# First attention of a four-layer kernel: closing token tiles by pairs inside the attention's last group, and writing the routing's column marks in four pieces

## The chip, the cores and the metric

The kernel runs on one core of a Trainium2 chip. The metric is the device time of one execution in microseconds, and where several runs are given, their median. All engines of the core take part: TensorE (PE; its weight loads are listed apart as PEld), VectorE (DVE), ScalarE (ACT), GpSimd (POOL) and SyncE (SP), which issues most of the DMA transfers. Lines such as L235 are lines of the kernel before the change.

## The reference

Four layers, each an attention and a feed-forward part, with a residual and a layer norm after each part. The state x has 1024 tokens of 256 numbers. Only the first layer matters here; what follows it is the same in both kernels.

```python
x = L0_attn_x
x = _layernorm(x + _L0_attn_ref(x, Wq, Wk, Wv, Wo, lam), axis=-1)   # (x - mean) / sqrt(var + 1e-5)
x = _layernorm(x + _L0_ffn_ref(x, Wr, Wg, Wu, Wd), axis=-1)
...
# _L0_attn_ref: 16 heads of 128 on 4 key heads, rotary angles, a window of 64 tokens;
# the probabilities are relu(softmax(q1 k1) - lam * softmax(q2 k2)), made to sum to 1
# _L0_ffn_ref: 8 experts of 256 x 256, two for each token
router_logits = jnp.einsum('bsh,he->bse', hidden_states, Wr)          # 1024 x 8
topk_logits, selected = jax.lax.top_k(router_logits, 2)
router_probs = jax.nn.softmax(topk_logits, axis=-1)
for e in range(8):
    w_e = jnp.where(selected == e, router_probs, 0.0).sum(axis=-1, keepdims=True)
    g = jnp.clip(jax.nn.silu(x @ Wg[e]), -7, 7)
    out = out + ((g * (x @ Wu[e])) @ Wd[e]) * w_e
```

## The kernel before

x lies in SBUF as eight tiles of 128 tokens (`k.x`), beside a transposed copy (`k.xT`) that the products read. The stages run one after the other (`STAGES`, L2145): attn0, ffn0, attn1 and so on. Each opens pools of its own, and a tile of a new pool whose memory was an old tile's waits until the old one was last read.

**attn0** (L513) goes through 32 units, four groups of four heads (g) by eight token tiles (t), in an order written out by hand (`in_order`). In one turn of its loop three units are worked on: unit i gets its scores (L666 and L676 on PE, the largest value by L684 on DVE, eight exponentials L692 on ACT), unit i-1 its difference of the two softmaxes (L700 to L708 on DVE, four relus L712 on ACT, the division L720 on POOL), and unit i-3 its product with the values: four transposes L729 on PE, a copy to `pt` L731 on ACT, L735 on PE, a copy to `ot` L741 on ACT, the output product L747 on PE, and L235 on DVE, which adds the result to x. While there are groups left, each turn also makes rotated queries and keys of the next half group (L154 on PE, L570 and L572 on DVE, L577 and L578 on POOL). In the last turns there is nothing left to make, and the units' own chain is alone. For g = 3 tile t of x is final when unit (3, t) has been added.

Loads are issued by SP in the order of the program. At the start these are x, the first keys, the rotary tables, weights, `lam` (L551), more weights, and then small tensors that later stages need, the first of them `bq` of attn1 (L1002), which DVE scales early (`scaled_bq`, L1004), ahead of the first unit's L684.

After the loop, `k.layernorm()` (L188) norms x by halves of four tiles: `bn_stats` and `bn_aggr` (L204, L205) for each tile, a square root on ACT (L222) and a reciprocal on DVE (L223) for four tiles together, then L208 on each tile. The function `four_layers` then turns all eight tiles with four calls of `transpose_two` (transposes L173 on PE, a copy L180 on DVE).

**ffn0** (L764) sends tokens to experts. Each token is put into two of 23 blocks of 128 slots, blocks belonging to one expert each.

- x is stored to DRAM by halves (`moe_rows`, L781), and the experts' weights are loaded: 24 transfers of 256 KB into `gu` (L787) and `wd` (L790), all on SP's queue. The second half's store stands in that queue behind the first eight of them. The first transfer waits for the last product of attn0 with the value tiles (L735), whose memory `gu` takes over.
- Routing: logits of all eight tiles (16 products of 128x8, L161 by way of `project_rows`), copied out by L817; the two largest for each token (`max` and `max_index`, L819 and L820); `chosen` as floats (L823); `mine` marks each token's experts (L824), `taken` sums them (L830). Two sorts of products (L833, L837) rank the tokens of an expert; L844 to L870 make of this the slot of each token, as a block and a column in it.
- `is_column` (L874, 128x2048 marks) and `is_block` (L879 to L886) are the operands of 16 products (L892) whose sum is the list of tokens by slot. `tokens` (L899) and `experts` (L909) come from it.
- 23 gathers by POOL (L228) fetch the rows of x by `tokens`, and then the blocks run: transposes (L927), the two hidden products (L938), the down product (L957).

The probabilities of a token's two experts (`prob`, L912 to L917) are not needed before the end of ffn0.

A later stage, attn3, already closes its tiles by pairs with a generator called `close`, with the inverse root as a power on POOL (`power`, L212: L215 on DVE, then L216 on POOL). The trace therefore has rows of such a closing.

Of the kernel before, what the change touches and what calls it, by code (L numbers as in the profile page):

```python
# [31 lines left out]
P = 128  # L32
T = 1024
NT = T // P
D = 256
# [477 lines left out]
def attn0(k, a):  # L513
# [89 lines left out]

    odd, even = [], []

    def make_values(t):
        vt = k.tile("v", [P, 512])
        ps = k.bank()
        k.project_rows(ps, lambda c: wv[:, c, :], t * P)
        nc.scalar.copy(vt, ps)  # L610
        odd.append(vt)
        vt = k.tile("v", [P, 512])
        if t == 0:
            nc.gpsimd.memset(vt[:64], 0.0)
        else:
            nc.sync.dma_start(out=vt[:64], in_=odd[t - 1][64:])
        nc.sync.dma_start(out=vt[64:], in_=odd[t][:64])
        even.append(vt)

    runs = [(g, half) for g in range(4) for half in range(2)]  # L620
    with k.in_order():
# [4 lines left out]
        for i in range(len(units) + 3):  # L626
# [7 lines left out]
            if i < len(units):  # L634
                g, t = units[i]
                if t % 4 == 0:
                    for _ in ahead:
                        pass
                    at = i // 4 + 1
                    ahead = operands(*runs[at]) if at < len(runs) else iter(())  # L640
                    if t == 0 and 0 < g < 3:
                        load(g + 1)
                next(ahead, None)
                if g == 0:
                    make_values(t)
            next(ending, None)
            if i < len(units):
                made[i] = attn0_probs(k, t, g, queries[g, t // 4], keys[g], lam)
# [115 lines left out]
def ffn0(k, a):  # L764
# [6 lines left out]
    blocks = 2 * T // P + 7  # L771
    gu = k.tile("gu", [P, 8, NC, 512])
    wd = k.tile("wd", [P, 8, NC, D])
    rows = k.tile("dram", [T, D], tag="moe_rows")
    results = k.tile("dram", [blocks * P, D], tag="moe_results")
    wr = k.weights([P, NC, 8], a["L0_ffn_Wr"].rearrange("(c p) e -> p c e", p=P))
    ternary_tiles = list(ffn1_weights(k, a))
    for tile_ in ternary_tiles[:2]:
        next(tile_)
    for half in range(2):  # L780
        nc.sync.dma_start(  # L781
            out=rows[half * HALF : (half + 1) * HALF, :].rearrange("(t p) d -> p t d", p=P),
            in_=k.x[:, 4 * half : 4 * half + 4, :],
        )
# [7 lines left out]
    def small(shape, dtype=F32):  # L792
        return k.tile("route", shape, dtype)
# [21 lines left out]
    logits, top = small([P, NT, 8]), small([P, NT, 8])  # L815
    which = small([P, NT, 8], U32)
    nc.vector.tensor_copy(logits, ps)  # L817
# [3 lines left out]
    chosen, mine = small([P, 2, NT]), k.tile("route", [P, 2, NT, 8], tag="mine", bufs=1)  # L821
    for i in range(2):
        nc.vector.tensor_copy(chosen[:, i, :], which[:, :, i])  # L823
    nc.vector.tensor_tensor(  # L824
        mine, cols[:, :8].unsqueeze(1).unsqueeze(1).to_broadcast([P, 2, NT, 8]),
        chosen.unsqueeze(3).to_broadcast([P, 2, NT, 8]), ALU.is_equal,
    )
    taken = small([P, NT + 1, 8], BF16)
    nc.vector.memset(taken[:, NT, :], 0.0)
# [20 lines left out]
    for i, by in enumerate((1, 2, 4)):  # L850
# [28 lines left out]
    nc.vector.tensor_tensor(  # L879
        hit.rearrange("p k t b -> p (k t) b"),  # L880
# [8 lines left out]
        )  # L889
    ps = k.bank()[:, : 2 * blocks].rearrange("p (i b) -> p i b", i=2)  # L890
    for i in range(2 * NT):
        nc.tensor.matmul(  # L892
            ps, lhsT=is_column[:, i, :], rhs=is_block[:, i // NT, i % NT],
            start=i == 0, stop=i == 2 * NT - 1,
        )
    low = small([P, blocks])
    nc.vector.tensor_copy(low, ps[:, 0, :])
    tokens = k.tile("route", [P, blocks], I32, tag="tokens", bufs=1)
    nc.vector.scalar_tensor_tensor(tokens, ps[:, 1, :], float(P), low, ALU.mult, ALU.add)  # L899

    passed = k.tile("route", [P, blocks, 7], tag="passed", bufs=1)
    nc.vector.tensor_tensor(
# [8 lines left out]
    prob = k.tile("const", [P, 2, NT], tag="prob")  # L911
    p1, p2 = prob[:, 0, :], prob[:, 1, :]  # L912
    nc.vector.tensor_tensor(p2, top[:, :, 1], top[:, :, 0], ALU.subtract)
# [1245 lines left out]
def four_layers(ctx: ExitStack, tc: tile.TileContext, a, out):  # L2159
# [88 lines left out]
```

## Time and profile before

| | |
|---|---|
| runs | 2280.4, 2282.05, 2284.7 us; median 2282.05 |
| the profiled execution's own time | 2276.97 us |
| its span, from the first to the last instruction | 2275.3 us |
| PE busy | 2065.0 us (91%), mean granted clock 0.965 |
| DVE, ACT, POOL busy | 58%, 38%, 23% |
| attn0's loop ends (last L235) | 294.5 us |
| first gather (L228) | 316.1 us |
| first expert's product (L938) | 322.1 us |

The profiled execution lies 5.1 us below the median of the runs. Times within it count from the start of the span. In the view of the stretches, each row is a piece of time with the busy time (and number of instructions) of PE, PEld, DVE, ACT and POOL, then the granted clock of PE as a share of full speed, the share of the DMA engines that is busy, and GB/s. In the timeline, a row is a start, a duration, an engine, a line and what it writes from what; a bracket tells for how long the engine had been idle and what it waited for. In the chain of waits a row is a start, a duration and an operation, each following what released it.

### The profile page before, as it was taken

The page shows a single profiled execution, that of the slowest core. Times are in us where ns is not written, and L with a number is a line of the kernel's source. Part 1 is how long each engine was busy: PE and PEld are TensorE (multiplying, and loading weights), DVE is VectorE, ACT ScalarE, POOL GpSimd, SP SyncE. Part 2 cuts the span into 40 slices and gives each one's busy share as a digit, 9 for nine tenths or more (in the row PEclk, how much of TensorE's full clock was granted, in tenths as well). Part 3 has the DMA queues.
Part 4 walks back from the last instruction along what each step waited for, and adds up shares of the span by engine and source line. Part 5 has one row for each costly group of instructions (what it writes and reads, how often), then busy time and mean ns, then how long its engine had stood idle before and what let it go on. Part 6 is the DMA issues. An engine that isn't in the chain of part 4 may idle for free.

```text
span 2275.3 us, 25208 instructions
## 1 busy us (share of the span) xinstructions
PE 2065.0 (91%) x7955; PEld 1211.8 (53%) x7955; DVE 1325.2 (58%) x2687; ACT 856.9 (38%) x2230; POOL 528.2 (23%) x805
## 2 busy tenths in 40 slices
PE   8999769799999997988888999899998778999997
PEld 4666545466676665754434444466666444444443
DVE  5677646567776777456744444476767774222223
ACT  3666624443343433444452224544443321111111
POOL 4333221333333333402110001333333220000000
PEclk9999879899999999979999999999999989999999
DMA  4100054254545544105000010244445441111100
GB/s 160 36 10 29 29 169 121 65 136 110 139 112 151 151 111 117 38 28 177 2 2 10 28 29 1 48 90 111 96 103 112 104 95 39 37 40 44 30 2 19
DMA packets 200804, 166.74 MB, mean 73 GB/s; under 512 B 71680, under 2 KB 176192, under 8 KB 200672
## 3 DMA queue, kind: packets, MB, share of 16 engines
q1 hardware_dynamic: 191088, 140.07, 24.0%
q0 software_dynamic: 9584, 25.05, 3.7%
q8 instruction: 65, 1.06, 0.2%
q14 instruction: 67, 0.55, 0.1%
HBM read 68.72 MB, written 17.17 MB: 38 GB/s over the span
## 4 chain that ended last, share of the span: by engine, by line
PE 67%; DVE 15%; ACT 6%; DMA 4%; issue 4%; POOL 2%; SPq 1%; DVEq 0%; ACTq 0%; POOLq 0%
PE bank L154 23%; PE wide L307 8%; PE wide L332 8%; PE bank L298 7%; PE bank L161 4%; DVE turned L276 3%; ACT e L692 3%; PE bank L758 2%; DMA pt<-turned 2%; PE bank L1107 2%; PE bank L1544 1%; PE bank L938 1%; PE bank L1282 1%; DVE st L684 1%; PE bank L747 1%
## 5 line engine op out<-in xcount | busy, mean ns | idle before, releaser
L154 PE MATMUL bank<-xT,w 128*128 128x512 f32 (+2 forms) x1520 | 659.8, 567 | 4.1 <-DVE xT L180 2.6
L154 PEld LDWEIGHTS bank<-xT,w 128*128 128x128 f32 (+1 forms) x1520 | 287.9, 194 | 272.6 <-issue 250.7
L276 DVE STREAM_TRANSPOSE turned<-p 128x128 f32<-128x128 f32 (+7 forms) x256 | 312.8, 1222 | 122.1 <-DMA pt<-turned 87.0
L307 PE MATMUL wide<-k,q 128*128 128x512 f32 (+3 forms) x768 | 294.1, 493 | 29.6 <-ACT p L253 28.7
L261 POOL TENSOR_SCALAR p<-p,st 128x128 f32<-128x128 f32 (+7 forms) x256 | 190.4, 744 | 503.0 <-DVE st L260 502.5
L298 PE MATMUL bank<-pt,v 128*128 128x256 f32 x1216 | 282.0, 375 | 7.5 <-DMA pt<-turned 5.0
L298 PEld LDWEIGHTS bank<-pt,v 128*128 128x128 f32 x1216 | 231.5, 194 | 61.9 <-issue 20.0
L307 PEld LDWEIGHTS wide<-k,q 128*128 128x128 f32 x768 | 141.2, 191 | 152.2 <-issue 93.6
L248 DVE TENSOR_REDUCE st<-wide 128x1 f32<-128x128 f32 (+7 forms) x256 | 194.1, 758 | 8.8
L253 ACT ACTIVATE p<-wide,st,factor 128x128 f32<-128x128 f32 (+7 forms) x128 | 106.4, 831 | 235.0 <-POOL st L250 223.7
L2138 DVE TENSOR_TENSOR t<-t,bank 128x512 f32<-128x512 f32 (+1 forms) x66 | 45.4, 688 | 251.6 <-PE bank L154 251.0
L332 PE MATMUL wide<-t,w 128*128 128x512 f32 (+1 forms) x392 | 187.3, 600 | 4.5 <-DVE t L2139 2.8
L253 ACT ACTIVATE p<-wide,st 128x128 f32<-128x128 f32 (+7 forms) x128 | 94.9, 741 | 249.5 <-DVE st L248 229.4
L2137 ACT ACTIVATE t<-bank 128x512 f32<-128x512 f32 (+1 forms) x66 | 39.4, 597 | 306.2 <-PE bank L154 306.2
L161 PE MATMUL bank<-w,xT 128*128 128x512 f32 (+3 forms) x320 | 124.6, 525 | 2.9 <-DVE xT L180 2.9
L243 DVE TENSOR_TENSOR wide<-wide,causal 128x128 f32<-128x128 f32 x256 | 74.2, 290 | 89.7 <-PE wide L307 88.5
L332 PEld LDWEIGHTS wide<-t,w 128*128 128x128 f32 (+1 forms) x392 | 68.2, 189 | 108.6 <-issue 48.1
L692 ACT ACTIVATE e<-wide,st 128x128 f32<-128x128 f32 x256 | 90.1, 377 | 50.9 <-DVE st L684 34.4
L1569 ACT ACTIVATE pt<-wide 128x1024 f32<-128x1024 f32 (+3 forms) x96 | 75.7, 811 | 72.2 <-PE wide L1563 69.9
L161 PEld LDWEIGHTS bank<-w,xT 128*128 128x128 f32 x320 | 59.2, 208 | 48.5 <-issue 42.7
L2131 POOL COPY t<-select 99x128 bf16<-99x128 bf16 (+1 forms) x33 | 9.4, 292 | 319.8 <-PE bank L988 319.8
L235 DVE TENSOR_TENSOR x<-bank,x 128x256 f32<-128x256 f32 x120 | 48.1, 412 | 50.6 <-PE bank L747 21.1
(310 smaller groups left out, 2864.0 us busy)
## 6 DMA issues: line engine op xcount, KB each, us to landing
pt<-turned SPq DMA_DIRECT2D x96, 128.0 KB, 2.8
pt<-turned SPq DMA_DIRECT2D x96, 96.0 KB, 2.4
pt<-turned SPq DMA_DIRECT2D x32, 256.0 KB, 4.9
w<-in_L_ffn_gate_up_dram SPq DMA_DIRECT2D x16, 512.0 KB, 3.7
pt<-turned SPq DMA_DIRECT2D x64, 112.0 KB, 2.5
pt<-turned SPq DMA_DIRECT2D x32, 224.0 KB, 4.4
w<-in_L_attn_Wq_dram SPq DMA_DIRECT2D x12, 512.0 KB, 4.3
w<-in_L_attn_Wo_dram SPq DMA_DIRECT2D x12, 512.0 KB, 3.8
```

What stands on the lines that cost most here:

```text
L154: self.nc.tensor.matmul(out, lhsT=weight(c), rhs=self.xcols(c, lo, n), start=c == 0, stop=c == NC - 1)
L161: self.nc.tensor.matmul(out, lhsT=self.xcols(c, lo, n), rhs=weight(c), start=c == 0, stop=c == NC - 1)
L243: nc.vector.tensor_tensor(scores[:, n - P : n], scores[:, n - P : n], self.causal, ALU.add)
L248: nc.vector.tensor_reduce(top, scores[:, :n], axis=AX.X, op=ALU.max, negate=True)
L253: nc.scalar.activation(probs[:, :n], scores[:, :n], AF.Exp, bias=top, scale=1.0 if scale is None else scale, accum_out=total,)
L261: self.nc.gpsimd.tensor_scalar(probs[:, :n], probs[:, :n], total, 1.0, ALU.mult, ALU.mult)
L276: nc.vector.transpose(squares[:, slot if both else 0], probs[:, :n].rearrange("p (k i b) -> p b k i", b=4, i=32),)
L298: self.nc.tensor.matmul(out[:, first * P :].rearrange("p (s q) -> p s q", q=32), lhsT=value, rhs=pt[:, first * 4 :, b * 32 : b * 32 + 32], ...
L307: self.nc.tensor.matmul(s[:, lo : lo + m], lhsT=query, rhs=key(lo, m), start=True, stop=True)
L332: nc.tensor.matmul(acc[m][:, half * HALF : (half + 1) * HALF], lhsT=down[:, m * P : (m + 1) * P], rhs=h, start=i == 0, stop=i == count - 1,)
L692: nc.scalar.activation(e[:, r, f, b, :], sc[:, r, f, b, :], AF.Exp, bias=top[:, at : at + 1], accum_out=total[:, at : at + 1],)
L1569: nc.scalar.activation(two[:, :, lo:], sc[:, :, lo:], AF.Exp)
```

## The change

- `close(t)` is a new generator in attn0 that closes tiles t and t+1 in four steps: statistics and the inverse root (by `power`, so DVE and POOL in the place of ACT's square root); norm, and a store of the two tiles to `moe_rows`; transposes; logits of the two tiles with the two largest, their indices as floats in `chosen`, and the difference of the largest in `prob`. Its tiles are in pools of attn0.
- A closing is queued when a unit of g = 3 with odd t has been added. `close_on` takes one step of the oldest closing; the loop calls it twice a turn, and after the last turn the rest is run to its end. In the program's order, tiles 0 and 1 and tiles 2 and 3 are closed between the last units; tiles 4 and 5 have their norm ahead of the last L235 and their transposes and logits behind it; tiles 6 and 7 come whole behind that.
- The router's weights `wr` (256 pieces of 32 bytes) are loaded at the start of attn0, in SP's order after the seventh weight and ahead of the last three early weights and `bq`; before, this load stood later, and was issued at 82.3 us. They lie in a tile of their own, no longer in the ring of ten `w` tiles.
- The layer norm after attn0, the four `transpose_two` ahead of ffn0, the two stores of halves, and the logits in ffn0 are gone. The store of tiles 6 and 7 stands in SP's queue behind the first eight weights of the experts, as the second half's did; that of tiles 4 and 5 behind the first one.
- In ffn0, `is_column` is written in four pieces of 128x512. The first stands ahead of `is_block` in DVE's order, the other three behind it. `expert` is summed ahead of `hit`, `experts` stands ahead of the list's copy `low`, and the rest of `prob` is made around `taken`, the first of it between `mine` and `taken`.
- No ACT square root is left in attn0's end, and with it go two table loads (ahead of L222 and of the exponential L914).

```diff
+    wr = k.tile("const", [P, NC, 8], tag="wr")
+    nc.sync.dma_start(out=wr, in_=a["L0_ffn_Wr"].rearrange("(c p) e -> p c e", p=P))
+    k.moe_rows = k.tile("dram", [T, D], tag="moe_rows")
+    k.chosen = k.tile("const", [P, 2, NT], tag="chosen")
+    k.prob = k.tile("const", [P, 2, NT], tag="prob")
+
+    def close(t):
+        stats = k.tile("st", [P, 4, 2], tag="stats", bufs=2)
+        for i in range(2):
+            k.add_stats(t + i, stats)
+        rstd = k.power(stats[:, t % 4 : t % 4 + 2, 1], 2, LN_EPS, tag="root")
+        yield
+        for i in range(2):
+            k.norm_tile(t + i, stats, rstd[:, i : i + 1])
+        nc.sync.dma_start(
+            out=k.moe_rows[t * P : (t + 2) * P, :].rearrange("(t p) d -> p t d", p=P),
+            in_=k.x[:, t : t + 2, :],
+        )
+        yield
+        k.transpose_two(t)
+        yield
+        ps = k.bank()[:, :16].rearrange("p (t e) -> p t e", t=2)
+        for i in range(2):
+            k.project_rows(ps[:, i, :], lambda c: wr[:, c, :], (t + i) * P)
+        logits, top = (k.tile("st", [P, 2, 8]) for _ in range(2))
+        which = k.tile("st", [P, 2, 8], U32)
+        nc.vector.tensor_copy(logits, ps)
+        for i in range(2):
+            nc.vector.max(top[:, i, :], logits[:, i, :])
+            nc.vector.max_index(which[:, i, :], top[:, i, :], logits[:, i, :])
+        for i in range(2):
+            nc.vector.tensor_copy(k.chosen[:, i, t : t + 2], which[:, :, i])
+        nc.vector.tensor_tensor(
+            k.prob[:, 1, t : t + 2], top[:, :, 1], top[:, :, 0], ALU.subtract
+        )
+        yield
+
+    closing = []
+
+    def close_on():
+        if closing and next(closing[0], k) is k:
+            closing.pop(0)
...
+            close_on()
             next(ending, None)
             if i < len(units):
                 made[i] = attn0_probs(k, t, g, queries[g, t // 4], keys[g], lam)
...
             if i - 1 in made:
                 made[i - 1] = next(made[i - 1])
+            close_on()
             for _ in ending:
                 pass
+            if i >= 3 and units[i - 3][0] == 3 and units[i - 3][1] % 2:
+                closing.append(close(units[i - 3][1] - 1))
+        while closing:
+            close_on()
...
-    wr = k.weights([P, NC, 8], a["L0_ffn_Wr"].rearrange("(c p) e -> p c e", p=P))
-    for half in range(2):
-        nc.sync.dma_start(
-            out=rows[half * HALF : (half + 1) * HALF, :].rearrange("(t p) d -> p t d", p=P),
-            in_=k.x[:, 4 * half : 4 * half + 4, :],
-        )
...
-    ps = k.bank()[:, : NT * 8].rearrange("p (t e) -> p t e", t=NT)
-    for t in range(NT):
-        k.project_rows(ps[:, t, :], lambda c: wr[:, c, :], t * P)
-    nc.vector.tensor_copy(logits, ps)
-    for t in range(NT):
-        nc.vector.max(top[:, t, :], logits[:, t, :])
-        nc.vector.max_index(which[:, t, :], top[:, t, :], logits[:, t, :])
...
-    nc.vector.tensor_tensor(
-        is_column, cols.unsqueeze(1).to_broadcast([P, 2 * NT, P]),
-        column.unsqueeze(2).to_broadcast([P, 2 * NT, P]), ALU.is_equal,
-    )
...
     for i in range(2 * NT):
+        if i % 4 == 0:
+            nc.vector.tensor_tensor(
+                is_column[:, i : i + 4, :], cols.unsqueeze(1).to_broadcast([P, 4, P]),
+                column[:, i : i + 4].unsqueeze(2).to_broadcast([P, 4, P]), ALU.is_equal,
+            )
         nc.tensor.matmul(
...
-            mine = {attn1: (), ffn1: (), ffn2: (), attn2: (0, 2), ffn3: ()}
+            mine = {ffn0: (), attn1: (), ffn1: (), ffn2: (), attn2: (0, 2), ffn3: ()}
...
-            if stage in (attn0, attn1):
+            if stage == attn1:
                 k.layernorm()
```

More of the change, by code (lines that the diff above doesn't have):

```diff
@@ L773, in ffn0 @@
     wd = k.tile("wd", [P, 8, NC, D])
-    rows = k.tile("dram", [T, D], tag="moe_rows")
+    rows = k.moe_rows
     results = k.tile("dram", [blocks * P, D], tag="moe_results")
-    wr = k.weights([P, NC, 8], a["L0_ffn_Wr"].rearrange("(c p) e -> p c e", p=P))
     ternary_tiles = list(ffn1_weights(k, a))
@@ L809, in ffn0 @@
     nc.gpsimd.tensor_copy(place, part)
-    ps = k.bank()[:, : NT * 8].rearrange("p (t e) -> p t e", t=NT)
-    for t in range(NT):
-        k.project_rows(ps[:, t, :], lambda c: wr[:, c, :], t * P)
-    logits, top = small([P, NT, 8]), small([P, NT, 8])
-    which = small([P, NT, 8], U32)
-    nc.vector.tensor_copy(logits, ps)
-    for t in range(NT):
-        nc.vector.max(top[:, t, :], logits[:, t, :])
-        nc.vector.max_index(which[:, t, :], top[:, t, :], logits[:, t, :])
-    chosen, mine = small([P, 2, NT]), k.tile("route", [P, 2, NT, 8], tag="mine", bufs=1)
-    for i in range(2):
-        nc.vector.tensor_copy(chosen[:, i, :], which[:, :, i])
+    mine = k.tile("route", [P, 2, NT, 8], tag="mine", bufs=1)
     nc.vector.tensor_tensor(
         mine, cols[:, :8].unsqueeze(1).unsqueeze(1).to_broadcast([P, 2, NT, 8]),
-        chosen.unsqueeze(3).to_broadcast([P, 2, NT, 8]), ALU.is_equal,
+        k.chosen.unsqueeze(3).to_broadcast([P, 2, NT, 8]), ALU.is_equal,
     )
@@ L895, in ffn0 @@
         )
[L896 to L899, printed above, removed]
     passed = k.tile("route", [P, blocks, 7], tag="passed", bufs=1)
@@ L909, in ffn0 @@
     nc.vector.tensor_copy(experts, expert)
-    prob = k.tile("const", [P, 2, NT], tag="prob")
+    low = small([P, blocks])
+    nc.vector.tensor_copy(low, ps[:, 0, :])
+    tokens = k.tile("route", [P, blocks], I32, tag="tokens", bufs=1)
+    nc.vector.scalar_tensor_tensor(tokens, ps[:, 1, :], float(P), low, ALU.mult, ALU.add)
+    prob = k.prob
     p1, p2 = prob[:, 0, :], prob[:, 1, :]
-    nc.vector.tensor_tensor(p2, top[:, :, 1], top[:, :, 0], ALU.subtract)
     nc.scalar.activation(p2, p2, AF.Exp)
```

## Prediction

> **What bounds the kernel now.** I read the table of the profiled execution first, then the view of the stretches around attn0's end, then the chain of waits there, and last the timeline wherever an edit lands. Over the whole span PE is busy 91%; the change touches a hole in that. The stretches:
>
> ```profile
> 245.00:294.00 49.00, 35.00 (x182) 26.32 (x181) 22.64 (x73) 26.30 (x119) 7.91 (x13) 0.86 0.09 31
> 294.00:316.00 22.00, 9.93 (x74) 9.31 (x71) 14.55 (x72) 3.07 (x4) 0.00 (x0) 0.59 0.90 291
> 316.00:322.00 6.00, 1.35 (x4) 0.58 (x4) 0.85 (x2) 0.00 (x0) 4.69 (x5) 0.50 0.24 75
> ```
>
> From 294 to 322 us no compute engine is full: one chain runs, and beside it the DMA engines (0.90) load the experts. The chain of waits names it:
>
> ```profile
> 294.04 0.44 DVE x L235
> ...
> 297.74 2.46 PE bank L161 x14
> 300.19 0.73 PE bank L173 x3
> 300.93 3.65 PE bank L161 x18
> 304.60 0.23 DVE route L817
> ...
> 310.94 2.17 issue
> 313.11 0.55 DVE hit L879
> ...
> 314.48 0.79 PE bank L892 x16
> ...
> 316.09 1.25 POOL rows L228
> ```
>
> The reader is to see the logits of all eight tiles in two pieces (6.1 us, 32 passes of about 0.2 us), and 2.17 us called "issue" that is DVE writing `is_column` (one instruction of 2.29 us). All that follows hangs on the first gather (316.09) and the first expert (322.10): what is saved ahead of them is saved at the end.
>
> **The change, part by part.** The sum is made against the profiled execution's own 2276.97 us. Minus is a gain.
>
> **1. The start: +0.5.** `wr` is now ahead of `bq` in SP's queue, and `bq` is late already (timeline of DVE):
>
> ```profile
> 28.22 0.17 DVE L1004 TENSOR_SCALAR scaled_bq<-bq 128x16 f32<-128x16 f32 x1 [1.80 <-DMA bq<-in_L_attn_bq_dram]
> 28.42 1.23 DVE L684 TENSOR_REDUCE st<-wide 128x8 f32<-128x1024 f32 x1
> ```
>
> Behind DVE's wait for `bq` stands the first unit's L684, whose scores end at 28.40, and the chain runs through it. So only 0.2 us of a later `bq` are hidden. The trace does not show 256 pieces of 32 bytes in a full queue. Nearest rows: `bq`, `bk` and `bv`, 128 pieces each, issued at 20.17, 20.81 and 21.41, land after 8.0, 7.6 and 7.5 us, so 0.2 to 0.5 us apart: 0.5 to 1.0 us for 256. Farther: around `lam`'s 512 pieces of 8 bytes the DMA share is 0.2 to 0.6 for 5.5 us (14.0 to 19.5), so 2.75 us for 256. Below nothing is excluded, since only work is added. I take 0.7, the middle of the nearest rows, less 0.2: +0.5, ends 0 and +2.55.
>
> The Trainium skill, page "DMA: Bandwidth & Descriptors", section "Bandwidth", speaks against this edit: transfers under 64 KB are dominated by their descriptors, at some 10.5 ns a packet. By it 256 packets are an estimated 2.7 us, this term would be +2.5 and the sum -0.5; the rows of `bq` and `bk` (0.2 to 0.5 us for 128) are well below.
>
> **2. attn0's last turns: -0.6.** The closings of tiles 0 to 3 lie beside the units' chain. DVE's share for a pair, some 4.5 us (statistics 1.05, norm 0.74, copy 0.66, logits about 1.1, the rest small), fits into its idle times (3.53 us ahead of L684 at 257.3, 1.9 us ahead of three L700). PE's first four transposes (0.55 us) fit into its 2.4 us ahead of L735 at 262.07, and the first logits push only L747 and L729, which wait for nothing urgent. What changes is the end:
>
> ```profile
> 277.04 1.28 ACT L222 ACT_TABLE_LOAD   x1
> 278.33 0.30 ACT L222 ACTIVATE st<-st,eps 128x4 f32<-128x4 f32 x1
> ```
>
> Without these the relus wait for L708, which begins some 0.25 us sooner, since an L204 of 0.42 us ahead of it goes too. Its last piece is ready near 278.3, the last relu ends near 278.8 in the place of 279.79, and `ot` and L747 follow: -0.95. The second pair's logits stand ahead of tile 6's L735, in a gap of 0.73 us; eight such passes took 1.08 us at full clock in attn3's closing (1900.06): +0.35.
>
> The clock is the open cost. It fell to half at 270.7 and 280.9, each time for 3.4 us after a stretch in which PE was busy 1.2 to 1.5 us of 3.4; that cost 0.7 us in L676 (1.76, not 1.05) and 1.7 in L747 and L729 (3.23 and 1.06, not 1.99 and 0.60). The added passes may fill those stretches (-2.4) or fall into a half-clock piece themselves (+1.8). I take 0, as the dips may as well move: -0.6, ends -3.0 and +1.2.
>
> The Trainium skill, page "TensorE: Matmul & The Clock Gate", section "Part 1: The HAM clock gate", has the clock fall after an idle window of about 3.4 us and return after a busy one. Here it fell though PE was never idle for more than 2.4 us, and from 298.0 to 304.4 it stayed at 0.50 though PE was busy throughout with 8-column passes. By the rule there would be no dips to win and the ends of this term would shrink to it, with the same sum.
>
> **3. From the last L235 to `taken`: -2.2.** Now 294.46 to 307.60, 13.14 us. In the new order what remains is a chain of two pairs, since tiles 6 and 7 start their statistics behind the logits of 4 and 5. First pair: L180 0.76, eight passes 1.1, then copy 0.2, two tiles' largest 0.43 (eight took 1.72), floats and difference 0.45: 2.95. Second pair: statistics 1.05, L215 0.2, then L216, which this row of attn3's closing prices,
>
> ```profile
> 1896.53 0.72 POOL L216 TENSOR_TENSOR root<-root,minus_half 128x2 f32<-128x2 f32 x1 [19.22 <-DVE root L215]
> ```
>
> with hand-overs 0.85, norm 0.75, transposes 0.9, L180 0.75, eight passes 1.8 (0.21 each at half clock, as now), copy, largest and floats 0.9, and `mine`, the exponential that DVE now awaits (ACT 0.21, L915 0.17) and `taken` 0.75: 7.95. Together 10.9: -2.2. Ends: all passes at full clock -3.4, all at half -1.5.
>
> **4. From `taken` to the first gather: -0.4.** Now 8.49 us. Two of L915 to L917 go under the rank products, where DVE idles 0.66: -0.25. Of the 16 products L892 only four are left behind the last piece: 0.6 becomes 0.35. `experts` fits into that wait: -0.15. Four pieces at about 0.6 (L879 has 0.53 for 368 columns) are 2.4 for 2.2: +0.2. Ends: -0.7, and +0.3 if the products gain nothing.
>
> **5. Weights and gathers: +0.2.** The store of tiles 6 and 7 blocks SP's queue as this one does now:
>
> ```profile
> 297.70 0.36 SPq L781 DMA_DIRECT2D moe_rows<-x  x1
> ```
>
> Their norm ends 5.8 us (2.95+1.05+0.2+0.85+0.75) after the last L235, at 294.36+5.8: the store goes 2.5 us later, at 300.2. Behind it come 16 weights at 0.75 us (the pace from 304.4 to 308.2): last landing near 314, now 313. The first expert would run at 319.6 (322.1-2.5): a cover of over 5 us, and if it went, each us past 319.6 would cost one. The first gathers may meet the last weights; their landings spread from 2.7 to 4.5 us: +0.2, ends 0 (now they meet none) and +1.6.
>
> Sum: 0.5-0.6-2.2-0.4+0.2 = **-2.5**, so 2274.5 for the profiled execution; the runs' median stands 5.1 higher: 2279.5. All good ends give -7.1, all bad ones +4.2.
>
> **The rivals.** (B) The clock stays up: dips gone (-2.4) and part 3 at full clock (-1.2): -6.1, 2276.0. For it: PE's idle stretches get shorter; against: behind the last L747 PE still idles for 4 us. (C) The experts' weights become the bound: at the 170 to 250 GB/s of the slices from 295.2 to 296.4 us the 16 weights (4.2 MB) take 20 us and end near 321.3, which leaves -0.8: 2281.2. Against: all later slices show 340 to 360 GB/s. (D) Slower: `bq` comes late at the start. If `wr`'s pieces cost the whole of `lam`'s stretch, 5.5 us, then 5.3 take the place of 0.5: +2.3, 2284.4; from 3.2 us of delay on the kernel is slower than before. For it: the 0.2 us of cover; against: `bk` and `bv`. (E) The change doesn't do what it says: half the tiles still close behind the loop, the passes meet the half clock (part 2 +1.2, part 3 -1.5, part 4 0): +0.4, 2282.5.
>
> **How the numbers follow.** Forecast 0.55, B 0.22, C 0.06, D 0.10, E 0.07. A measurement of this kernel can tell about 0.2% (4.6 us) from no change. Faster by more: 0.20 of B and 0.04 of the forecast, 0.24. Slower by more: 0.06 of D and 0.01 each of C and E, 0.08. Within: 0.68. The range goes from all good ends nearly (2275.2) to D's price (2285.0).
>
> **What would show it.** Right: `bq` lands 0.5 to 1 us later; no L222 near 277; 10 to 11 us from the last L235 to `taken`; the last three pieces of `is_column` beside L892; the first expert waiting for its gather. Wrong: DVE waiting for `bq` past 30 us; a wait of L938 for `gu`; half clock through the last units.

## The result, and the profile after

The changed kernel takes 2279.09 us in the median of 20 runs (2270.29 to 2285.19), the kernel before 2280.4 in 20 runs (2272.9 to 2288.9). The ratio is 0.9987 with a 95% interval of 0.9977 to 0.9997: 3.0 us less, between 0.7 and 5.2 (the two medians alone differ by 1.3 us). Single runs of either kernel scatter by a standard deviation of 4 us, by 9 us at most, more than the change moves, so what follows is read from stretches within the traces, and from many executions.

The profiled execution of after has a span of 2277.7 us, 2.4 more than that of before, though its median is lower. The stretches around attn0's end show it (columns as before: busy us of PE, PEld, DVE, ACT, POOL, then granted clock, DMA share, GB/s):

```profile
245.00:297.00 52.00, 40.51 (x212) 31.30 (x211) 28.91 (x101) 26.13 (x124) 11.99 (x17) 0.84 0.11 31
297.00:317.00 20.00, 6.29 (x49) 4.85 (x47) 13.73 (x64) 1.49 (x2) 0.71 (x1) 0.58 0.92 290
317.00:323.00 6.00, 1.38 (x4) 0.58 (x4) 0.85 (x3) 0.00 (x0) 4.46 (x5) 0.50 0.50 154
```

attn0 ends at 297.0 in the place of 294.0, and the stretch from there to the first gather is 20 us in the place of 22. What is gained behind attn0 was lost in it, in this execution. Of the 2.97 us by which the last L235 is later, 0.34 are the start, 1.50 lie in the first three groups, whose program is the same, and 1.13 in the last turns. The start, in DVE's timeline:

```profile
28.68 0.17 DVE L1038 TENSOR_SCALAR scaled_bq<-bq 128x16 f32<-128x16 f32 x1 [1.99 <-DMA bq<-in_L_attn_bq_dram]
28.76 1.22 DVE L735 TENSOR_REDUCE st<-wide 128x8 f32<-128x1024 f32 x1
```

(L1038 and L735 are L1004 and L684 of before.) The wait for `bq` ends 0.46 us later, and the first unit's maximum follows it. The closing of the last four tiles, again DVE's timeline:

```profile
297.01 0.42 DVE L235 TENSOR_TENSOR x<-bank,x 128x256 f32<-128x256 f32 x1 [1.73 <-PE bank L798]
297.44 0.69 DVE L180 COPY xT<-bank 128x512 f32<-128x512 f32 x1
299.29 0.17 DVE L634 COPY st<-bank 128x16 f32<-128x16 f32 x1 [1.15 <-PE bank L161]
...
300.53 0.42 DVE L204 BATCH_NORM_STATS2 st<-x 128x6 f32<-128x256 f32 x1
...
302.73 0.73 DVE L208 TENSOR_SCALAR x<-x,stats,root 128x256 f32<-128x256 f32 x2 [0.83 <-POOL root L216]
...
307.12 0.17 DVE L634 COPY st<-bank 128x16 f32<-128x16 f32 x1 [1.97 <-PE bank L161]
...
308.79 0.22 DVE L864 TENSOR_TENSOR route<-mine 128x64 bf16<-128x64 f32 x1
```

The reader is to see two closings one behind the other: tiles 4 and 5 until 300.5, and only then the statistics of tiles 6 and 7, final since 297.4. From the last L235 (297.43) to `taken` (309.01) it is 11.58 us. The chain of waits of after is misleading in one place:

```profile
311.80 5.49 DMA wd<-in_L_ffn_Wd_dram
...
317.32 1.25 POOL rows L228
```

It puts the first gather down to the weight `wd`. But `tokens` is written until 317.01, and the gather starts 0.31 us behind `tokens` here as in the kernel before (315.78, 316.09): the weight landed in the same moment by chance.

### The profile page after: what moved, and what is told of

It is laid out like the page before. It is cut to its first block, busy times and chain, and to the rows that moved or that the text cites. A ratio compares the mean times of both kernels' runs of the same rounds, so it can differ in the third digit from the quotient of the medians.

```text
span 2277.7 us, 25229 instructions
## 1 busy us (share of the span) xinstructions
PE 2063.0 (91%) x7955; PEld 1209.7 (53%) x7955; DVE 1328.4 (58%) x2704; ACT 852.8 (37%) x2226; POOL 530.9 (23%) x809
## 4 chain that ended last, share of the span: by engine, by line
PE 65%; DVE 15%; ACT 6%; DMA 5%; issue 4%; POOL 2%; SPq 2%; DVEq 0%; ACTq 0%; POOLq 0%
PE bank L154 23%; PE wide L332 8%; PE wide L307 7%; PE bank L298 7%; DVE turned L276 4%; PE bank L161 3%; ACT e L743 3%; DMA pt<-turned 3%; PE bank L809 2%; SPq L284 2%; PE bank L1141 2%; PE bank L1578 1%; PE bank L972 1%; PE bank L1316 1%; DVE st L735 1%
## 5 line engine op out<-in xcount | busy, mean ns | idle before, releaser
L161 PE MATMUL bank<-w,xT 128*128 128x512 f32 (+2 forms) x288 | 118.5, 547 | 3.3 <-DVE xT L180 2.9
L161 PEld LDWEIGHTS bank<-w,xT 128*128 128x128 f32 x288 | 52.5, 196 | 48.8 <-issue 41.6
L1555 DVE TENSOR_REDUCE st<-wide 128x2 f32<-128x1024 f32 x64 | 64.3, 1020 | 18.8 <-PE wide L1551 9.4
```

The source lines that it names most:

```text
L161: self.nc.tensor.matmul(out, lhsT=self.xcols(c, lo, n), rhs=weight(c), start=c == 0, stop=c == NC - 1)
```

## The experiments

Two theories stand against each other. **Mine**: the stretches behind attn0 get shorter by fixed amounts, the start costs a little, and the later last L235 is the clock's chance. **The rival**: the closings between the last units are what makes attn0 later, and eat half of the gain. Three stretches are read from each trace: last L235 (its end) to the end of `taken`, from there to the first gather, from there to the first expert's product; "sum" is these three. A fourth column has the last three turns of attn0, from one L235 to the last (start to start), where the closings between the units would cost. Ratios are to the kernel before on the same chip.

| | last three turns | L235 to taken | to gather | to expert | sum | ratio (95%) |
|---|---|---|---|---|---|---|
| before | 18.89 | 13.14 | 8.49 | 6.01 | 27.64 | |
| before, again | 23.16 | 11.88 | 8.50 | 6.05 | 26.43 | |
| after | 18.01 | 11.58 | 8.31 | 5.99 | 25.88 | 0.9987 (0.9977 to 0.9997) |
| load of wr moved | 17.97 | 11.59 | 8.32 | 5.98 | 25.89 | 0.9987 (0.9973 to 1.0) |
| many pieces | 17.63 | 11.59 | 8.31 | 6.05 | 25.95 | 0.9991 (0.9977 to 1.0005) |
| no lost step | 19.72 | 8.08 | 8.31 | 5.94 | 22.33 | 0.9982 (0.9967 to 0.9996) |
| whole marks | 17.62 | 11.59 | 8.43 | 5.94 | 25.96 | 0.9977 (0.9961 to 0.9994) |
| single end | 19.85 | 5.23 | 8.31 | 7.94 | 21.48 | 0.9994 (0.9974 to 1.0013) |
| store by ACT | 19.71 | 5.29 | 8.31 | 8.32 | 21.92 | 0.9978 (0.9961 to 0.9996) |
| square root | 15.80 | 11.22 | 8.31 | 5.97 | 25.50 | 1.0012 (0.9997 to 1.0026) |
| fill | 18.63 | 11.59 | 8.32 | 5.93 | 25.84 | 0.9986 (0.9968 to 1.0004) |
| wr by ACT | 19.15 | 11.59 | 8.32 | 6.14 | 26.05 | 0.9987 (0.9976 to 0.9999) |
| held weights | 19.74 | 5.26 | 8.32 | 5.92 | 19.50 | 0.9965 (0.9954 to 0.9976) |
| together | 19.85 | 6.91 | 8.32 | 6.03 | 21.26 | 0.9978 (0.9961 to 0.9995) |

In the executions of the changed order the first stretch repeats within 0.01 us, the second too, the third within 0.2; in the two of before the first differs by 1.26. The last three turns depend on where the clock is at half (below). The ratios of 12 runs (20 for after) do not tell neighbours apart.

**The load of wr, moved in the program.**

```diff
-    nc.sync.dma_start(out=wr, in_=a["L0_ffn_Wr"].rearrange("(c p) e -> p c e", p=P))
...
+            if i == 8:
+                nc.sync.dma_start(
+                    out=wr, in_=a["L0_ffn_Wr"].rearrange("(c p) e -> p c e", p=P)
+                )
```

> The changed kernel with the load of wr issued in turn 8 of the unit loop, behind the early loads, so that SP's queue at the start is that of the kernel before. Theory (the start costs +0.5, about 0.3 of it from the queue): DVE's wait for bq ends at 28.2 again in the place of 28.7, the first unit's L735 maximum starts at 28.4 and not 28.76, and the kernel is 0.3 us faster than the changed one, too little for the medians. Rival (the 0.3 us are chance of this one execution, lam came late as well): the wait still ends between 28.2 and 28.7, no different. Rival D (wr's pieces hold the queue for several us): would show as 2 us or more and is already unlikely, as the profile after has DVE waiting for bq only 0.2 us longer than before.

The edit did nothing: SP issued `wr` at 12.43, and at 12.25 without the edit. The section fixes the order of the compute engines alone; SP's order is that of a planner, which orders at build time what the program leaves free, and not the program's. So it is no test of the start. It is a second execution of the changed kernel's instructions, and as such the best evidence on the clock. The same two turns of the last group in after and in this run, as stretches:

```profile
259.57:270.40 10.83, 9.42 (x43) 7.61 (x44) 5.31 (x23) 6.55 (x35) 1.04 (x1) 0.64 0.19 51
270.40:279.00 8.60, 7.50 (x38) 5.47 (x36) 4.52 (x17) 3.70 (x18) 1.00 (x1) 0.67 0.00 0
```

```profile
260.95:268.11 7.16, 5.74 (x43) 4.72 (x44) 5.28 (x23) 5.14 (x28) 1.04 (x1) 1.00 0.29 76
268.11:275.12 7.01, 5.17 (x38) 3.84 (x36) 4.61 (x18) 4.99 (x27) 1.00 (x1) 1.00 0.00 1
```

The same 43 and 38 passes take 10.83 and 8.60 us at a mean clock of 0.64 and 0.67, and 7.16 and 7.01 at 1.00.

**wr by ACT.** The load is issued by `nc.scalar` at the same place, where ACT's order is the program's.

> The changed kernel with wr's load issued by ACT in turn 8 of the unit loop, so that it no longer stands in SP's queue ahead of bq (the run meant to do this by moving the statement left the load where it was, as SP's order is the planner's). Theory (wr's 256 pieces cost bq some 0.5 us, as 1024 more pieces made it land 2.0 us later): bq is issued at 20.2 in the place of 21.1 and DVE's wait for it ends at 28.0 to 28.3, while the eight runs with wr early had 28.41 to 28.94; the first unit's maximum starts at 28.4, unless lam's own chain is later. Rival (the 0.3 us are chance): the wait ends between 28.4 and 28.9 as in the others.

`bq` is issued at 20.17 (21.12 in after), and DVE's timeline has

```profile
28.31 0.17 DVE L1041 TENSOR_SCALAR scaled_bq<-bq 128x16 f32<-128x16 f32 x1 [1.88 <-DMA bq<-in_L_attn_bq_dram]
28.43 1.22 DVE L738 TENSOR_REDUCE st<-wide 128x8 f32<-128x1024 f32 x1
```

Over all executions the first maximum starts at 28.42, 28.36, 28.43 and 28.33 without the early load, and at 28.49 to 29.06 in nine with it (mean 28.76; the run with many pieces is left out): +0.4 us. My theory holds, the size is the forecast's.

**Many pieces.**

```diff
+    for n in range(4):
+        more = k.tile("rope", [P, NC, 8], tag=f"more{n}", bufs=1)
+        nc.sync.dma_start(out=more, in_=a["L0_ffn_Wr"].rearrange("(c p) e -> p c e", p=P))
```

> The changed kernel with wr's load issued five times ahead of bq, into tiles of their own that nothing reads: 1024 more pieces of 32 bytes in the queue at the start, to price them. By the nearest rows of the prediction (0.5 to 1.0 us for 256 pieces, from bq, bk and bv): bq lands 2 to 4 us later, at 30.7 to 32.7. By the row of lam (2.75 us for 256), and by the Trainium skill's page 'DMA: Bandwidth & Descriptors', section 'Bandwidth', as an estimate: 11 us later, near 39. The kernel is later by the same amount, since the first unit's maximum stands behind the wait for bq; if the kernel is not later by what bq is, the chain had slack that was overlooked.

The wait for `bq` ends at 30.66: 2.0 us later than in after for 1024 pieces, 0.5 for 256, the low end of the nearest rows. The rest of the expectation failed, and usefully: the kernel is not later, since the planner put `scaled_bq` behind the first maximum (28.69) now. A late `bq` costs only as much as the planner's order leaves in its way. In the changed kernel `scaled_bq` does stand ahead of the first maximum; what refutes rival D there is the 0.46 us.

**No lost step.** The call that finds a closing at its end uses up a turn's step. The edit removes the last `yield` of `close`:

```diff
             k.prob[:, 1, t : t + 2], top[:, :, 1], top[:, :, 0], ALU.subtract
         )
-        yield
```

> The changed kernel without the empty last step of each closing. In the changed kernel the call that finds a closing at its end does nothing else, so of the steps of tiles 4 and 5 two (transposes, logits) are left for behind the last product. Without it they stand inside the last turn and only tiles 6 and 7 close behind the loop. Theory (the time from the last L235 to taken is a chain of two pairs, of which the first takes 3.2 us): that stretch shrinks from 11.58 to 8.2 to 8.9 us, the last turns stay within 0.5 us, since PE idles for 4 us there, and the kernel is 2 to 3.3 us faster than the changed one. Rival (the last turns have no room: the copy of the transposes on DVE and eight products of 8 columns on PE stand ahead of the last output product): the last L235 comes 1.1 to 1.9 us later and the gain is 1 to 1.5 us. Rival (the experts' weights bound as soon as routing is faster): the first expert waits for gu or wd, and the gain ends at about 4 us.

The stretch goes from 11.58 to 8.08, 3.5 less, and the last turn stays 5.03 us: as the theory has it. But the last three turns pay for it. They take 19.71 to 19.85 us in all five executions without the lost step, and 17.62 to 18.01 in four of the changed order; a fifth has 19.15, with 6.9 us at half clock as the five, where the four have 3.4. PE's timeline shows the third turn from the end, which takes 9.40 us in the place of 7.58 to 8.39:

```profile
279.86 1.88 PE L161 MATMUL bank<-wr,xT 128*128 128x8 f32 x8 [0.78 <-DVE xT L180]
...
281.59 3.76 PE L797 MATMUL bank<-w,ot 128*128 128x256 f32 x8
```

The logits (L161), which in the changed kernel stand behind the output product (L797 here), stand ahead of it now and push it. From the start of these three turns to the first expert's product it is 42.47 us, and 44.00 to 44.31 in the four: 1.5 to 1.8 us are left of the 3.5 (3.1 by the fifth, 45.62). That lies between my theory (2 to 3.3) and the rival, no room in the last turns (1 to 1.5); whether the longer stretch at half clock is the edit's doing, which all five have with it and one of five without, is not shown. The ratio's gain over after (0.0005, 1.1 us) agrees, though it is smaller than its interval.

**Whole marks.** `is_column` in one instruction ahead of `hit`, the four pieces gone.

> The changed kernel with is_column written whole ahead of hit again, the rest as changed: prices the four pieces alone. Prediction's step 4 had them at -0.05 (2.2 by 2.4 us of DVE, and twelve of the sixteen products beside DVE), the other -0.35 from experts, prob and the list's order. Theory: the time from taken to the first gather goes from 8.31 to 8.4, within 0.2 us either way, and the kernel is the same. Rival (the pieces are what pays, the order of the rest nothing): 8.31 becomes 8.5 or more. Rival (the pieces cost, since each waits for its start): it falls to 8.1 or less.

From `taken` to the gather 8.43, and 8.31 with the pieces: they are worth 0.12 us, and the rest of the new order 0.06 (8.49 to 8.43).

**Single end.** Without the lost step, and tiles 6 and 7 closed one by one (`close(t, n)`, with one-tile transposes):

```diff
+            if i == len(units) + 2:
+                six = close(6, 1)
+                next(six)
             close_on()
...
-        while closing:
-            close_on()
+        seven = close(7, 1)
+        for part in (seven, six, six, seven, seven, six, seven, seven):
+            next(part, None)
```

> As the run without the empty step, and beyond that tiles 6 and 7 close one by one: tile 6's statistics and norm stand inside the last turn, its transposes and logits beside tile 7's statistics; the store of tiles 6 and 7 together stays on SP's queue, behind seven of the experts' weights. Theory (one chain through statistics, root, norm, transposes, copy, logits, largest): what is left behind the last L235 is that of one tile, 0.6+0.2+0.85+0.4+0.5+0.45+0.95+0.2+0.45+0.4+0.3+0.4 = 5.7 us in the place of 8.08 for two and 11.58 in the changed kernel; the gather starts 8.3 us after that as before. Rival C (the experts' weights bind): in the changed kernel the last weight landed some 21.4 us after the last L235, the first expert would now start 20 us after it; then the first expert's product waits for gu or wd and 1 us or more of the 2.4 are lost. Rival (tile 6's steps delay the last product): the last turn, 5.0 us from L235 to L235, becomes 5.5 or more.

L235 to `taken` is 5.23, better than expected, and the last turn stays 5.02: tile 6's steps do not delay the last product. But from gather to expert it is 7.94 in the place of 6. PE's timeline there, and the stretch before it:

```profile
314.46 1.15 PE L981 MATMUL bank<-ident,rows 128*128 128x128 f32 x4 [6.78 <-DMA rows<-moe_rows,tokens]
```

```profile
310.00:312.00 2.00, 0.00 (x0) 0.00 (x0) 0.00 (x0) 0.00 (x0) 1.70 (x2) 0.50 1.10 348
312.00:314.00 2.00, 0.00 (x0) 0.00 (x0) 0.00 (x0) 0.00 (x0) 1.39 (x3) 0.50 0.94 309
```

The gather, started at 308.43, feeds PE 6.03 us later (3.03 in after), once the weights' 350 GB/s end. Rival C is right here, but by another road than expected: not the expert waits for its weights, the gather waits among them.

**Store by ACT.** `nc.scalar` issues the store of tiles 6 and 7.

> The run that closes tiles 6 and 7 one by one, with their store on ACT's queue in the place of SP's, so that no weight waits behind it. Theory (the first expert waits for its gather, weights have cover): the same times within 0.1 us in every stretch, though the last weight lands 2 to 3 us sooner. Rival C: the first expert starts sooner by what it waited for weights in the run with the store on SP, 1 us or more. Also possible: weights and the store of tiles 6 and 7 share the DMA engines, the store lands later and the first gather, which reads it, waits for it.

The first two stretches are the same, the third is 0.4 us worse, and the last weight did not land sooner as expected: here too the weights fill the DMA engines (busy share 0.94 to 1.14 from 306 to 314 us), and the gather feeds PE 6.04 us after its start. So it is not the store in SP's queue that makes the gather late.

**Held weights.** The single end, and four of the eight `wd` loads behind the first block's transposes:

```diff
         turned(0)
+        nc.vector.memset(wd[0:1, 4:8, 0, 0:1], 0.0)
+        for e in range(4, 8):
+            nc.sync.dma_start(
+                out=wd[:, e], in_=a["L0_ffn_Wd"][e].rearrange("(c p) h -> p c h", p=P)
+            )
```

> The run that closes tiles 6 and 7 one by one (store on SP), with the down weights of four experts held back: a DVE write of one number into each of their places, behind the copy of the first block's transposes, comes ahead of their loads. Theory (there the first gather, issued at 308.4, landed only at 314.4 because the DMA engines were full of weights until 313.5: 7.9 us from gather to first expert in the place of 5.95): with 1 MB, about 3 us, of weights out of its way the gather takes 2.8 to 3.5 us again, and gather to first expert goes to 6.0 to 6.6; the down weights land some 10 us before or at the first down product, and from the last L235 to the first expert it is 19.6 to 20.2 us, 1.3 to 1.9 less than there and 5.8 less than in the changed kernel. Rival (the gather is late for another cause, its store of tiles 6 and 7 above all): 7.9 stays. Rival (what is held back is missed later): the first down product, 7.9 us after the first expert's product in the kernel before, waits for wd.

Gather to expert is 5.92 again. In PE's timeline the rows are there 3.43 us after the gather's start (310.29):

```profile
313.72 0.69 PE L984 MATMUL bank<-ident,rows 128*128 128x128 f32 x2 [4.18 <-DMA rows<-moe_rows,tokens]
...
316.21 2.05 PE L995 MATMUL bank<-gu,xT 128*128 x2 [0.75 <-DVE xT L989]
```

From the last L235 to the first expert it is 19.50 us, 6.4 less than in the changed kernel, and the ratio to before is 0.9965 (0.9954 to 0.9976), 8 us: this version beats both kernels. With the last three turns counted it is 39.66 us to the first expert, 4.3 to 4.7 less than the 44.00 to 44.31 of the changed order, and 46.95 and 50.01 in the two executions of before. No down product waits for `wd`; the first comes 8.2 us behind the first expert's product (7.7 before).

**Square root.** `k.rsqrt` in the place of `k.power` in all four closings.

> The changed kernel with ACT's square root and DVE's reciprocal in the place of the power on POOL in each of the four closings. Prices the part of prediction's step 2 that comes from leaving the square root out (two table loads of 1.28 us for each closing, at most eight). Theory (ACT is on the units' chain in the last turns): each of the three closings inside the turns holds ACT for 2 x 1.28 + 0.3 us, of which about half is on the chain: the last L235 comes 3 to 4.5 us later than it would (the clock's dips move it by up to 5 us as well, so the L235-to-L235 turns are to be compared: 5.0 to 5.2 us become 6 to 7); behind the last L235 nothing is lost, since the load runs while ACT has nothing to do: 11.58 stays within 0.5. Rival (loads fall into ACT's idle times): turns stay at 5.0 to 5.3 us and the kernel is the same.

Three turns became 7.85, 8.44 and 10.29 us at full clock, where they have 6.81, 7.16 and 7.01 with the power; 1.8 us of it came back in the next turn (5.76, with the power 7.6), and the kernel is probably slower than with the power (1.0012 by 0.9987, intervals that just meet at 0.9997). In sum that is 3.8 us, within the 3 to 4.5 expected, though not in the turns of 5 us that I had named. There were four table loads for the roots and exponentials, not eight: no exponential stands between the later closings. Behind the last L235 the square root is even 0.37 us faster than the power (11.22 by 11.59).

**Fill.** Eight transposes of the identity more in each turn of the last group, beside PE's waits for `pt` and `ot`:

```diff
+    if g == 3:
+        spare = k.bank()
+        for i in range(4):
+            nc.tensor.transpose(spare[:, i * P : (i + 1) * P], k.ident, k.ident)
```

(and once more, into the same bank, ahead of the output product)

> The changed kernel with eight transposes of the identity more in each turn of the last group, into a bank that nothing reads, placed where PE waits for pt and for ot: PE is busy some 1.2 us longer in each turn of about 5 us. Tells whether the half-clock windows in the last group come from PE's idle time. Theory (the clock falls after a stretch with PE busy less than half): no half-clock window between 265 and 290 us, where the runs so far had one of 3.4 us at least and 13.5 us at most; the last L235 then comes near 291.5, the earliest seen so far, and the median of the runs is 1 to 3 us below that of the changed kernel. Rival (dips do not depend on PE's share): windows are still there, the fill is doubled inside them, and the last L235 is later, by up to 1 us a window.

One half-clock window of 3.4 us is still there (277.3 to 280.7), as in the two best of the runs without a fill, and the median tells nothing. My expectation failed, but the theory behind it did not. The square-root run seems to speak against it, since the clock stayed at 1.00 through a turn in which PE was busy half of the time (busy us of PE first):

```profile
269.00:279.40 10.40, 5.25 (x39) 3.92 (x37) 4.72 (x20) 8.35 (x39) 1.04 (x1) 1.00 0.00 1
```

A turn is the wrong stretch to read, though. In each trace the changes of the clock lie on a raster of 3.41 us, to 0.1 us: in that of before at 250.2, 257.05, 270.65, 274.1, 280.9, 284.35 and 297.95. Where the raster lies differs between executions. PE's busy share in single steps of it:

| execution | step of the raster | PE busy | clock in the next step |
|---|---|---|---|
| before | 267.26 to 270.68 | 43% | 0.50 |
| before | 274.09 to 277.50 | 55% | 1.00 |
| before | 277.50 to 280.92 | 38% | 0.50 |
| square root | 269.84 to 273.25 | 65% | 1.00 |
| square root | 273.25 to 276.67 | 74% | 1.00 |
| square root | 276.67 to 280.08 | 9% | 0.50 |
| fill | 270.44 to 273.85 | 100% | 1.00 |
| fill | 273.85 to 277.27 | 38% | 0.50 |

So the fill did not reach the step that mattered: its transposes were through at 273.95, and PE then waited for `pt` until 275.56. Over the fourteen traces, from 243 us to the last L235, the clock fell 21 times, each time after a step with PE busy 9 to 49%. Of 140 steps after which it stayed up, 138 have 50% or more, two 45%. Behind the last L235, where PE does passes of 128x8, it also fell after steps of 55 to 76%, so the busy share is not the whole rule there.

**The kernel before, again.**

> The kernel before, unchanged, once more. Theory (the time of attn0's turns differs from run to run by the place of the half-clock windows, and the rest is fixed): from the last L235 to taken 13.1 us, from taken to the first gather 8.5, from there to the first expert 6.0, each within 0.1 us; the turns of the last group between 6.8 and 11 us each, at other places than in the first execution, and the last turn 5.02 us; the last L235 anywhere from 291.5 to 297. Rival (the later last L235 of the changed kernel, 297.0 by 294.0, is the closings' doing): 294.0 within 0.3 again.

The last L235 comes at 295.82 and not at 294.04, with a turn at half clock throughout. With the changed order it lies between 291.56 and 297.01 in five executions (median 292.67), so the closings do not make it later: where attn0 ends differs by chance with the half-clock stretches, and the rival falls. But one of my stretches fell too: L235 to `taken` is 11.88, not 13.14. Its chain of waits shows why:

```profile
299.51 1.46 PE bank L161 x14
...
301.45 3.66 PE bank L161 x18
```

In the first execution the first piece took 2.46 us. The clock falls 2 to 5 us after the last L235 in the fourteen traces, and it is chance whether those passes still get the full clock.

**Together.** Held weights, `wr` by ACT, and the square root for tile 7 alone.

> The run with tiles 6 and 7 closed one by one and four down weights held back, with two edits more: wr's load issued by ACT in turn 8 (bq's wait then ended at 28.31 in the place of 28.4 to 29.0), and ACT's square root with DVE's reciprocal for tile 7 alone in the place of the power (with the square root in all closings the stretch from the last L235 to taken was 11.22 and not 11.58, as nothing else runs on ACT there). Theory: bq's wait ends at 28.2 to 28.4; from the last L235 to taken 4.9 in the place of 5.26; from taken to the first gather 8.3, from there to the first expert 5.9 to 6.1; in sum 19.1 to 19.3 from the last L235 to the first expert, where the changed kernel has 25.9 and the kernel before 26.4 and 27.6. Against the kernel before, the ratio is 0.9955 to 0.9970. Rival (the exponential's table load, 1.28 us, now falls between mine and taken): 6.0 or more from the last L235 to taken. Rival (what is gained ahead of the experts is lost behind them, on SP's queue, which blocks on the held weights): the ratio is 0.998 or more although the first expert is earlier.

The start is as expected (28.24), the rest is not: 6.91 to `taken`, 1.65 more than with the power, and a ratio of 0.9978, above the 0.9955 to 0.9970 expected. ACT's timeline:

```profile
294.53 1.28 ACT L222 ACT_TABLE_LOAD   x1 [3.27 <-DVE stats L205]
295.82 0.29 ACT L222 ACTIVATE root<-stats,eps 128x1 f32<-128x1 f32 x1
```

ACT had been idle for 3.27 us, and the table load began only when the statistics were there: here it waited with its activation. The norm is 1.2 us later for that; another 0.3 are tile 7's logits, at half clock here (1.02 us, 0.72 with the power). In the square-root run the table was still loaded from the closing before. The expectation had the wrong load as its rival: the exponential's (1.28 us at 296.14) is hidden, as it ran 4 us ahead of the exponential itself (300.14).

## Why the prediction came out as it did

The sum (-2.5) is close to the measured -3.0, but the interval of the latter is 4.5 us wide, and the steps were not all right. That the forecast median of 2279.5 meets the measured 2279.09 is luck in part: it was counted from a median of three runs (2282.05), which lies 1.65 us above that of 20 (2280.4).

| step | forecast | measured |
|---|---|---|
| 1 start | +0.5 | +0.4 |
| 2 last turns | -0.6 | about -1.2, dips apart |
| 3 last L235 to `taken` | -2.2 | -1.6 and -0.3, by the two executions of before |
| 4 `taken` to gather | -0.4 | -0.2 |
| 5 weights and gathers | +0.2 | 0 (5.93 to 6.14, before 6.01 and 6.05) |

The measured terms add up to -1.3 to -2.6, which lies within the runs' interval of -5.2 to -0.7.

**Step 1** was right in mechanism and size. The Trainium skill's page "DMA: Bandwidth & Descriptors", section "Bandwidth", by whose 10.5 ns a packet I had estimated 2.7 us for the 256 pieces, gave more than five times the delay of `bq` (0.4 to 0.5 us). The many-pieces run has 2.0 us for 1024, some 2 ns each. These are delays of a later load and not the pieces' own time; part of that may lie in gaps of the DMA engines, which were 0.41 to 0.75 busy from 14 to 24 us in that run.

**Step 2**: the square root's removal was worth more than the 0.95 taken, and the +0.35 for the logits ahead of tile 6's values was not paid (the last two turns are 5.02 us each where the clock is full). The turn with L222 took 8.43 and 9.73 us in before at mean clocks of 0.84 and 0.73; in the changed order it takes 7.6 to 8.0 at 0.77 to 0.79 and 8.4 at 0.68 (9.4 where the lost step is gone and logits stand in this turn). On the line through the two of before, the first four are 1.1 to 1.7 less at the same clock, an estimate. The dips were rightly taken as open, and what goes ahead of them (PE busy less than half) was read rightly from two of them; their size was not: -2.4 to +1.8 was given, and two executions of the changed kernel's instructions differ by 5.3 us in these eight turns (60.35 and 55.06).

**Step 3** was the mis-sized one, in two terms. "Now 13.14 us" was read from one execution as if it were fixed; the other has 11.88. And the new chain takes 11.58, not 10.9: the first pair 3.10 (2.95 forecast), the second 8.48 (7.95). Of the second pair's 0.53, 0.4 is the piece behind the passes, "copy, largest and floats 0.9", which takes 1.33 (307.08 to 308.41). What I did not see in the change is the lost step: without it the whole first pair (3.5 us) goes from behind the loop, of which up to 2 us come back inside it, so the ending that I priced was one that the edit need not have had.

**Step 4**: the pieces gained 0.12 and the rest of the order 0.06, half of what was forecast. They take 0.68+1.89 = 2.57 us of DVE, not 2.4.

**Step 5**: the store of tiles 6 and 7 is issued 6.1 us after the last L235 (5.8 forecast), and the weights' traffic ends about 4.5 us ahead of the first expert. The cover was there. The weights become the bound, as rival C had it, once the chain is shorter by somewhere between 3.5 us (no lost step: 5.94 to the expert) and 6.4 us (single end: 7.94).

Of the signs, no L222, the pieces beside L927 (L892 before) and the first expert's wait for its gather came as said; the 10 to 11 us did not (11.58), and half clock through the last units, named as a sign against, came by the place of the raster.

## What to carry to other kernels

Where half-clock windows move from run to run, one trace prices a stretch of PE work only for that execution; take the stretches at equal clock, and from a second execution, before a difference of 1 us is believed. Read PE's busy share on the raster of the clock's own changes, not by turns. When a generator is stepped from a loop, count the calls that only find it ended: one of them kept 3.5 us of work behind the loop here. But look at the whole stretch before the gain is booked: inside the loop up to 2 us of it were paid again. When a chain ahead of a gather is shortened, look at what fills the DMA engines at the new time: shortening it by another 2.85 us made the first gather take 6.03 us to its use in the place of 3.60, until 1 MB of weights was held back.

## What the runs showed of the hardware that was not expected

- The granted clock falls to 0.50 for 3.4 us or a multiple, on a raster of 3.41 us that lies elsewhere in each execution of the same instructions. In attn0's last turns all 21 falls came after a step of the raster with PE busy 9 to 49%, and none after one with 50% or more. That the share is the cause is argued from these counts; no run here has raised the share in such a step. The Trainium skill's page "TensorE: Matmul & The Clock Gate", section "Part 1: The HAM clock gate", ties the fall to an idle window; in these turns a window less than half busy was followed by it too.
- An ACT table load of 1.28 us (294.53) began only when its activation's input was ready, though ACT had been idle for 3.27 us; the next one in the same run (296.14) ran 4 us ahead of its activation. What decides stays open.
- Behind full DMA engines (350 GB/s), the first gather took 6.03 us from its start to PE's use of the rows; 3.0 to 3.6 where the engines came free sooner.
